# A two-layer attention kernel: float32r sums, a moved output, and a last projection in two parts

## The chip, the cores and the metric

The kernel runs on one core of a Trainium2 chip. The metric is the device time of one execution in microseconds (us); lower is better. The core's engines are called by the names that the profile uses: PE is TensorE (matmuls; PEld its weight loads), DVE is VectorE, ACT is ScalarE, POOL is GpSimd, and SP is SyncE, which in this kernel only starts DMAs.

## The reference

Eight images of 32 x 32 positions and 512 channels go through two layers. Each layer is a group norm (32 groups of 16 channels), an attention and a residual. Everything is float32.

```python
x = x + L0(gn(x))          # 16 heads of 32: softmax(q k^T / sqrt(32)) v, then w_proj, b_proj
x = x + L1(gn(x))          # 4 heads of 128, then Wo

# L1, for each image (1024 tokens):
q = x @ Wq * scale; k = x @ Wk; v = x @ Wv
scores = q k^T + pos       # pos: relative logits from q and pos_emb_w, pos_emb_h
out = softmax(scores) @ v @ Wo
```

The softmax's denominator, a sum over 1024 keys for each head and query, is what the first part of the change touches.

## The kernel before

**Layout.** Activations lie with features on the partitions: an image is four chunks of 128 channels x 1024 tokens, in one of eight equal buffers ("block"). Logits are computed transposed, keys on the partitions and queries along the row, so the sum over keys runs over partitions. DVE therefore adds the exp tiles of the eight key blocks of a head into one tile `esum` (128 x 512 queries, L675 and L677), and TensorE multiplies that with a matrix of ones, which gives the sum in every partition.

**Projections.** Each of the ten or so 512 x 512 projections of an image uses a Strassen-Winograd form: instead of eight products of half size there are seven (`seven`, order 0, 5, 1, 4, 6, 2, 3), for each half `u` of the output features. `forms` makes on DVE, in four subtractions or additions (L339 to L342), the combinations of the four quarters of the activations; products 0 and 1 use raw quarters (`a11`, `a12`). A product is eight matmuls of 128 x 32 columns (`by_columns`, L315), four of them side by side in the array. Sinks (`Plain`, `Onto`) put the products' sums where they belong, with ACT copies (L374, L393), DVE adds (L379, L443) and POOL adds (L438). The weights, or sums of them, come by a planned stream of loads on SP's queue (`Stream`, L193 and L197); `Matrix.add_up` makes the summed weights once (L146) and stores them to DRAM.

**PSUM.** Eight banks: four are one tile "ps" (the layer-0 logits, four heads at once), three are "bank", one is "acc".

**Order of the work.** In the main loop pass b runs the layer-0 attention of image b (512 steps) and puts between its steps a list of other work: the end of layer 0 of image b−1 (`after_0`), the last projection of layer 1 of image b−2 (`after_1`, ending in `put_out`: transpose, then four stores for each tile, L856 and L861) together with the second norm of b−1, then q, k, v and the position logits of layer 1 of b−1 (`second`), its attention (`attention_1`), and the projections of layer 0 of b+1. The loading and first norm of b+1 (`load`) is woven between the steps of `attention_1`, one part every six steps (`woven(..., 4, 6)`). The steps of `attention_1` have cost 0 to the interleaver, so a whole second-layer attention normally runs within one step of the first-layer attention, and the "ps" banks are unused meanwhile. Only in the pass of the last image do the first 32 of its 64 steps alternate with layer-0 steps. The last pass has the second layer of image 7 alone, and after it the last projection, `after_1(7)`. A scheduler, which estimates durations, then decides each engine's final order within what the dependencies allow.

**A second-layer attention** has 4 heads x 2 halves of the queries, each of eight key blocks. A step (`front`, `back`) is a matmul q k (L654), a float32r matmul that adds the position logits (L655), an exp on ACT (L657), a matmul with v into "acc" (L666) and the DVE addition to `esum`. After the eighth, ACT copies acc to q's place (L680) and `finish` makes the sum:

```python
su = bank(f"sums_{name}")
nc.tensor.matmul(su, ones, esum, start=True, stop=True)     # L686
normalise(q[:, h, c * NB : (c + 1) * NB], su, name)
```

`normalise` copies it on ACT (L502), transposes it on DVE so that the reciprocal works on 16 columns (L504, L507), makes a check (L510), transposes back (L520) and multiplies on POOL (L524). These small tiles share tag "rec" with two buffers.

**The start** (`load_first`): image 0 is read in rows and transposed by TensorE; ACT and DVE copy the chunks out of PSUM (L752, L754); six idle matmuls follow; DVE takes statistics in chunk order 1, 0, 3, 2; `put_away` stores the four chunks to DRAM on SP's queue (L218); the group norm overwrites them in place (L294). The summed weights of the first projections are made on POOL and DVE (L146).

At the end of the kernel a flag is computed from the checks (L1014 to L1018): a slower general path would follow if a sum were out of bounds.

Of the kernel before, what the change touches and what calls it, by code (L numbers as in the profile page):

```python
# [17 lines left out]
P = 128  # L18
# [9 lines left out]
def quick_path(  # L28
# [55 lines left out]

    ident = consts.tile([P, P], F32, tag="ident", name="ident")
    make_identity(nc, ident)
    ones = consts.tile([P, P], F32, tag="ones", name="ones")
    nc.gpsimd.memset(ones, 1.0)
    bproj_sb = consts.tile([P, CC], F32, tag="bproj_sb", name="bproj_sb")
    with nc.allow_non_contiguous_dma(reason="512 values, once"):  # L90
        nc.gpsimd.dma_start(bproj_sb, b_proj.rearrange("(cc p) -> p cc", p=P))
# [71 lines left out]


    ORDER = [0, 5, 1, 4, 6, 2, 3]

    class Stream:

# [138 lines left out]

    begun = [None]
    half_done = [None]

    def by_columns(out, weights, moving, start, stop, open_sum=False):

# [11 lines left out]
                tc.keep_in_program_order(ins)  # L324
        in_place[0] = False

    def forms(x, name, room=None):


        a11, a12 = x[:, :HC, :NB], x[:, HC:, :NB]  # L330
        a21, a22 = x[:, :HC, NB:], x[:, HC:, NB:]
        if room is not None:
            s1, s2, s4 = [room[:, i, :].rearrange("p (c n) -> p c n", n=NB) for i in range(3)]
        else:
            s1, s2, s4 = [
                mem.tile([P, HC, NB], F32, tag=f"form{i}", name=f"f{i}_{name}", bufs=1)
                for i in (1, 2, 4)
            ]
        nc.vector.tensor_add(s1, a21, a22)  # L339
        nc.vector.tensor_sub(s2, s1, a11)  # L340
        nc.vector.tensor_sub(a21, a11, a21)
        nc.vector.tensor_sub(s4, a12, s2)  # L342
# [5 lines left out]
    def seven(fs, u, rows, sink, name, hook=None):  # L348

        def product(out, i, start):
            w, f = stream.take(i), fs[i]
            if not rows:
                for c in range(HC):
                    by_columns(out, w[c], f[:, c, :], start and c == 0, c == HC - 1, True)
            else:
                for t in range(2):
                    for c in range(HC):  # L360
                        by_columns(
                            out[:, t * HN : (t + 1) * HN],
                            f[:, c, (2 * u + t) * P : (2 * u + t + 1) * P],
                            w[c],
                            start and c == 0 and t == 0,
                            c == HC - 1,
                            True,
                        )
            stream.ahead()

        x = bank(f"x_{name}")
# [7 lines left out]
        begun[0] = nc.vector.tensor_add(a, y, p1)  # L379
# [23 lines left out]
        yield HC  # L403

    class Plain:

# [234 lines left out]
                if i % 2:  # L641
                    yield 0

    def attention_1(q, k, v, posT, b):

        steps = [(h, c, j) for h in range(H1) for c in range(NH) for j in range(NT)]
        state = {}

        def front(h, c, j):
            name = f"1_{b}_{h}_{c}_{j}"  # L650
            ps = bank(f"ps_{name}")
            keys = slice(j * P, (j + 1) * P)
            queries = slice(c * NB, (c + 1) * NB)
            nc.tensor.matmul(ps, k[h][:, keys], q[:, h, queries], start=True, stop=False)  # L654
            nc.tensor.matmul(ps, sel_flat[:, keys], posT[:, h, queries], start=False, stop=True)  # L655
            e = mem.tile([P, NB], F32, tag="e1", name=f"e_{name}", bufs=3)
            nc.scalar.activation(e, ps, AF.Exp, scale=1.0 / math.sqrt(D1))  # L657
            return e

        def back(h, c, j, e):  # L660
            name = f"1_{b}_{h}_{c}_{j}"
            if j == 0:
                state["acc"] = bank(f"acc_{name}")
                state["first"] = e
            acc = state["acc"]
            nc.tensor.matmul(  # L666
                acc,
                v[:, j, h * D1 : (h + 1) * D1],
                e,
                start=(j == 0),  # L670
                stop=(j == NT - 1),
            )
            if j == 1:
                state["esum"] = mem.tile([P, NB], F32, tag="es1", name=f"es_{name}", bufs=2)
                nc.vector.tensor_add(state["esum"], state["first"], e)  # L675
            elif j > 1:
                nc.vector.tensor_add(state["esum"], state["esum"], e)  # L677
            if j < NT - 1:
                return
            nc.scalar.copy(q[:, h, c * NB : (c + 1) * NB], acc)  # L680
            state["ended"] = (h, c, state["esum"])

        def finish(h, c, esum):
            name = f"1_{b}_{h}_{c}"
            su = bank(f"sums_{name}")
            nc.tensor.matmul(su, ones, esum, start=True, stop=True)  # L686
            normalise(q[:, h, c * NB : (c + 1) * NB], su, name)

        pending = None
        for at in steps:  # L690
            e = front(*at)
            ended = state.pop("ended", None)
            if pending is not None:
                back(*pending)
            pending = (*at, e)
            if ended is not None:
                finish(*ended)
            yield 0
        back(*pending)
        yield 0  # L700
        finish(*state.pop("ended"))

    def load(b, st):

# [15 lines left out]
        yield 0  # L720
        st["kept"] = put_away(xT, f"0_{b}")
        yield from group_norm(st, xT, f"0_{b}")
        st["xn"] = forms(x, f"xn0_{b}")
        yield 0

    def load_first(st):

# [7 lines left out]
        for h in range(NH):  # L735
# [6 lines left out]
            for t in range(NT // NH):  # L742
                for cc in range(CC):
# [2 lines left out]
                        rows[:, h * (NT // NH) + t, cc * P : (cc + 1) * P],  # L746
                        ident,
                    )
            for cc in range(CC):
                part = xT[cc][:, h * NB : (h + 1) * NB]  # L750
                if h == 0 or cc % 2:
                    nc.scalar.copy(part, banks[cc])  # L752
                else:
                    nc.vector.tensor_copy(part, banks[cc])  # L754

        idle = psum.tile([P, CC, NB], F32, tag="ps", name="idle", bufs=1)
        for t in range(6):
# [86 lines left out]

    def after_1(b, st, hook=None):

        if "ao1" not in st:
            forms_1(b, st)
        fs = st.pop("ao1")
        xT = fetch(st["kept"], block(f"x2T_{b}"))  # L850
        for u in range(2):

            def put_out(n, h):
                m = n * HC + u
                ot = mem.tile([P, NB], F32, tag="row", name=f"ot_{b}_{m}_{h}", bufs=3)
                nc.vector.transpose(ot, xT[m][:, h * NB : (h + 1) * NB])  # L856
                ot = ot.rearrange("p (t i) -> p t i", i=32)
                for a in range(P // 32):

                    queue = nc.scalar if b == B - 1 and a % 2 else nc.sync  # L860
                    queue.dma_start(  # L861
                        by_blocks(of[b, h * NB : (h + 1) * NB, :], m * P + 32 * a),
                        ot[32 * a : 32 * a + 32],
                    )

            stream.unit(WO, False, u)
            yield from seven(
                fs, u, False, Onto(halves(xT, u), then=put_out), f"wo_{b}_{u}", hook if u else None
            )

    def woven(main, side, start, gap, places=(0,)):

# [51 lines left out]
    for b in range(B + 1):  # L924
# [10 lines left out]
    plan += units(WO)  # L935
# [22 lines left out]
    for b in range(B + 1):  # L958
# [11 lines left out]
        if last is not None:  # L970
# [14 lines left out]
            attention = later(lambda st: attention_1(*st.pop("at")), last)  # L985
            if here is not None and coming is None:

                attention = woven(
                    (int(at < H1 * NT) for at, _ in enumerate(attention)),
# [513 lines left out]
```

## Time and profile before

| | |
|---|---|
| three timed runs | 3873.93, 3877.97, 3879.32 us; median 3877.97 |
| the profiled execution | 3877.0 us, of which the traced span is 3875.2 us |
| granted TensorE clock, mean | 0.996 of full speed |
| DVE, largest lines | L569 893.3 us (layer-0 sums), L677 290.6 us, 384 times, 757 ns each |
| ACT, largest lines | L547 961.6 us (layer-0 exp), L657 305.7 us, 512 times, 597 ns each |
| float32 sums of layer 1, L686 | 64 sums as 128 matmul records, 593 ns each |

Busy times of a line are sums of durations, and a share of 98% says that an engine nearly always had something in work. Matmuls are pipelined: the record of a matmul lasts longer than the distance to the next one, so what a matmul costs is read from the distance of starts, not from its duration. A float32 matmul has two records. The waits view lists, for an engine, the idle time before its instructions and what ended it; the timeline lists instructions in order of start, with that idle time in brackets.

### The profile page before, as it was taken

The numbers are of one execution on the slowest core, as the hardware profiler recorded it, in microseconds if no ns is written. First come the engines' busy times: TensorE is split into PE (matmuls) and PEld (weight loads), VectorE is DVE, ScalarE is ACT, GpSimd is POOL, SyncE is SP. The second block draws the span as 40 slices with busy tenths as digits, with TensorE's granted clock in tenths as the row PEclk, the third lists the DMA queues.
The fourth block names the chain that finished last, engine by engine and source line by source line (L and its number), as shares of the span: only waits on it lengthen the run. The fifth ranks groups of instructions, "written<-read, shape, count | busy, mean of one in ns | idle before, by whom it ended". The sixth has DMA issues, their size and how long they took to land.

```text
span 3875.2 us, 79813 instructions
## 1 busy us (share of the span) xinstructions
PE 3803.0 (98%) x34478; PEld 1375.0 (35%) x34478; DVE 2516.4 (65%) x2905; ACT 1723.9 (44%) x1767; POOL 625.1 (16%) x400
## 2 busy tenths in 40 slices
PE   8999999999999999999999999999999999999998
PEld 3222244232443234432343323433234332334353
DVE  6777765686745867468664686656866568665544
ACT  2554543545434454344544445444453445553232
POOL 2242101121001211012111121111210112001101
PEclk9999999999999999999999999999999999999999
DMA  6122120142202322033120241103311023110401
GB/s 183 58 87 80 42 60 3 37 126 65 57 6 79 94 54 55 12 92 87 42 55 17 92 94 38 47 21 98 90 41 39 27 97 76 34 52 24 121 17 23
DMA packets 482984, 234.73 MB, mean 61 GB/s; under 512 B 269600, under 2 KB 461376, under 8 KB 481600
## 3 DMA queue, kind: packets, MB, share of 16 engines
q1 hardware_dynamic: 470992, 213.74, 20.4%
q0 software_dynamic: 2608, 13.70, 1.0%
q8 instruction: 274, 4.49, 0.5%
q10 hardware_dynamic: 9024, 2.10, 0.3%
q14 instruction: 86, 0.70, 0.1%
HBM read 170.72 MB, written 58.72 MB: 59 GB/s over the span
## 4 chain that ended last, share of the span: by engine, by line
PE 87%; DVE 8%; ACT 2%; issue 2%; DMA 0%; SPq 0%; POOL 0%; DVEq 0%; ACTq 0%; POOLq 0%
PE ps L539 12%; PE ps L654 11%; PE acc L666 11%; PE acc L558 11%; PE y_q L315 4%; PE y_v L315 4%; PE y_k L315 4%; PE ps L655 3%; PE x_q L315 3%; PE z_k L315 3%; PE x_v L315 3%; PE x_k L315 3%; PE z_q L315 3%; PE z_v L315 3%; DVE es L569 2%; ACT e L547 2%
## 5 line engine op out<-in xcount | busy, mean ns | idle before, releaser
L547 ACT ACTIVATE e<-ps 128x2048 f32<-128x2048 f32 x512 | 961.6, 1878 | 839.3 <-PE ps L539 628.2
L569 DVE TENSOR_TENSOR es<-es,e 128x2048 f32<-128x2048 f32 x384 | 893.3, 2326 | 408.6 <-ACT e L547 405.6
L539 PE MATMUL ps<-q,k 32*64 32x512 f32 x8192 | 576.6, 614 | 18.4 <-ACT e L547 18.4
L657 ACT ACTIVATE e<-ps 128x512 f32<-128x512 f32 x512 | 305.7, 597 | 573.8 <-PE ps L655 537.8
L558 PE MATMUL acc<-e,v 128*32 128x512 f32 x4096 | 545.9, 605 | 0.0
L654 PE MATMUL ps<-q,k 128*128 128x512 f32 x1024 | 525.2, 595 | 0.3 <-DVE posT L640 0.3
L666 PE MATMUL acc<-e,v 128*128 128x512 f32 x1024 | 522.0, 593 | 0.0
L524 POOL TENSOR_TENSOR q<-q,su 128x512 f32<-128x512 f32 x128 | 216.3, 1690 | 1556.8 <-DVE su L520 1538.0
L677 DVE TENSOR_TENSOR es<-es,e 128x512 f32<-128x512 f32 x384 | 290.6, 757 | 252.8 <-ACT e L657 250.8
L655 PE MATMUL ps<-posT,sel 128*128 128x512 f32 x512 | 407.0, 795 | 0.0
L654 PEld LDWEIGHTS ps<-q,k 128*128 128x128 f32 x1024 | 192.9, 190 | 250.4 <-issue 243.8
L539 PEld LDWEIGHTS ps<-q,k 32*64 32x64 f32 x8192 | 120.3, 130 | 409.8 <-issue 221.1
L666 PEld LDWEIGHTS acc<-e,v 128*128 128x128 f32 x1024 | 193.5, 190 | 146.3 <-issue 105.0
L558 PEld LDWEIGHTS acc<-e,v 128*32 128x32 f32 x4096 | 81.5, 108 | 412.0 <-issue 364.7
L567 DVE TENSOR_TENSOR es<-e,e 128x2048 f32<-128x2048 f32 x64 | 172.9, 2701 | 33.2 <-ACT e L547 33.2
L504 DVE STREAM_TRANSPOSE tu<-su 128x512 f32<-128x512 f32 x128 | 90.6, 708 | 121.7 <-ACT su L502 120.1
L502 ACT COPY su<-sums 128x512 f32<-128x512 f32 x128 | 74.9, 585 | 149.0 <-PE sums L579 81.2
L655 PEld LDWEIGHTS ps<-posT,sel 128*128 128x128 f32 x512 | 97.5, 190 | 122.3 <-issue 122.3
L640 DVE TENSOR_TENSOR posT<-pp,posT 32x512 fp32r<-32x512 f32 x128 | 112.0, 875 | 32.3 <-ACT posT L635 31.0
L675 DVE TENSOR_TENSOR es<-e,e 128x512 f32<-128x512 f32 x64 | 44.2, 691 | 135.8 <-ACT e L657 135.8
L428 POOL TENSOR_TENSOR k<-b_k,p_k 128x512 f32<-128x512 f32 x32 | 51.9, 1623 | 483.6 <-ACT p_k L393 483.6
L635 ACT CAST posT<-pp 32x512 fp32r<-32x512 f32 x128 | 106.2, 829 | 46.3 <-PE pp L622 45.1
(200 smaller groups left out, 4449.4 us busy)
## 6 DMA issues: line engine op xcount, KB each, us to landing
w_qkv<-ws_qkv SPq DMA_DIRECT2D x168, 128.0 KB, 2.5
d<-x0T SPq DMA_DIRECT2D x32, 512.0 KB, 3.6
x1T<-d SPq DMA_DIRECT2D x32, 512.0 KB, 5.4
d<-x1T SPq DMA_DIRECT2D x32, 512.0 KB, 3.4
x2T<-d SPq DMA_DIRECT2D x32, 512.0 KB, 6.0
w_qkv<-in_L_conv_w_qkv SPq DMA_DIRECT2D x126, 128.0 KB, 2.2
out<-ot SPq DMA_DIRECT2D x240, 64.0 KB, 2.0
xs<-in_x SPq DMA_DIRECT2D x224, 64.0 KB, 2.5
```

The costliest lines, as they stand in the source:

```text
L315: ins = nc.tensor.matmul(out[columns, :], weights[:, columns], moving, start=start, stop=stop, skip_group_check=open_sum,)
L524: nc.gpsimd.tensor_tensor(dst, dst, su, op=ALU.mult)
L539: nc.tensor.matmul(ps[some, r, :], k[m][rows, j * P + 64 * i : j * P + 64 * i + 64], q[m][rows, h * NB : (h + 1) * NB], start=True, stop=True,
L547: nc.scalar.activation(e, ps, AF.Exp, scale=D0 ** -0.5)
L558: nc.tensor.matmul(acc[r * D0 : (r + 1) * D0, :], v[:, j, c0 : c0 + D0], e[:, r, :], start=(j == blocks[0]), stop=(j == blocks[-1]),)
L567: nc.vector.tensor_add(state["esum"], state["first"], e)
L569: nc.vector.tensor_add(state["esum"], state["esum"], e)
L654: nc.tensor.matmul(ps, k[h][:, keys], q[:, h, queries], start=True, stop=False)
L655: nc.tensor.matmul(ps, sel_flat[:, keys], posT[:, h, queries], start=False, stop=True)
L657: nc.scalar.activation(e, ps, AF.Exp, scale=1.0 / math.sqrt(D1))
L666: nc.tensor.matmul(acc, v[:, j, h * D1 : (h + 1) * D1], e, start=(j == 0), stop=(j == NT - 1),)
L677: nc.vector.tensor_add(state["esum"], state["esum"], e)
```

## The change

1. `ones` becomes a float32r tile. In `attention_1.finish` the sum of a head is split: ACT copies `esum` to float32r (`greater`), DVE subtracts that from `esum` (`rest`), and some steps later two float32r matmuls add both into a tile of the "ps" banks. `normalise` is the same. Only where the layer-0 attention of the last image alternates with the steps (`beside` = 32, that is for the first three sums of image 6) does the single float32 matmul into a "bank" stay. The sum at the very end of each attention is made at once, in all its parts.
2. `forms` becomes a generator, `forming`; in `load` its four operations are spread over four parts, each held behind the latest `esum` addition, and `load` gets a part every five steps.
3. At the start all eight copies out of PSUM are on ACT, in chunk order 0, 2, 1, 3, as are the statistics; the summing of the query and key weights of layer 0 is held behind the last of the forms.
4. The output of image 6 (`put_out`) is put off: its eight transposes with their stores come between the steps of the last attention.
5. The last projection of image 7 (`after_last`) makes products 0 and 1 for both halves u first, from raw quarters, then the forms, then the other five products for both halves; the plan of weights follows that order.

```diff
-    ones = consts.tile([P, P], F32, tag="ones", name="ones")
-    nc.gpsimd.memset(ones, 1.0)
+    ones_r = consts.tile([P, P], F32R, tag="ones", name="ones")
+    nc.gpsimd.memset(ones_r.bitcast(F32), 1.0)
+    ones = ones_r.bitcast(F32)
...
+    FIRST_TWO, LAST_FIVE = [0, 1], [5, 4, 6, 2, 3]
...
-    def forms(x, name, room=None):
+    def forming(x, name, room=None, behind=None):
...
+            late = behind() if behind is not None else None
+            with tc.issue_after(late.ins) if late is not None else nullcontext():
+                last_form[0] = op(out, one, other)
+            yield 0
...
+    def two_first(fs, u, sink, name):
+        product = taken(fs, u, False)
+        x = bank(f"x_{name}")
+        product(x, 0, True)
+        p1 = snapshot("e1", f"p1_{name}")
+        nc.scalar.copy(p1, x)
+        product(x, 1, False)
+        sink.c11(x)
+        return p1
+
+    def five_last(fs, u, sink, name, p1):
+        product = taken(fs, u, False)
+        y = bank(f"y_{name}")
+        product(y, 5, True)
+        a = snapshot("es1", f"a_{name}")
+        nc.vector.tensor_add(a, y, p1)
+        sink.early(p1, a)
...
         def finish(h, c, esum):
             name = f"1_{b}_{h}_{c}"
-            su = bank(f"sums_{name}")
-            nc.tensor.matmul(su, ones, esum, start=True, stop=True)
+            if (h * NH + c + 1) * NT < beside:
+                su = bank(f"sums_{name}")
+                nc.tensor.matmul(su, ones, esum, start=True, stop=True)
+                normalise(q[:, h, c * NB : (c + 1) * NB], su, name)
+                return
+            yield
+            greater = mem.tile([P, NB], F32R, tag="rec", name=f"sg_{name}", bufs=2)
+            nc.scalar.copy(greater, esum)
+            rest = mem.tile([P, NB], F32R, tag="rec", name=f"sr_{name}", bufs=2)
+            nc.vector.tensor_sub(rest, esum, greater.bitcast(F32))
+            yield
+            yield
+            su = psum.tile([P, HB, NB], F32, tag="ps", name=f"sums_{name}", bufs=1)[:, 0, :]
+            nc.tensor.matmul(su, ones_r, greater, start=True, stop=False)
+            nc.tensor.matmul(su, ones_r, rest, start=False, stop=True)
             normalise(q[:, h, c * NB : (c + 1) * NB], su, name)
...
-        finish(*state.pop("ended"))
+        run(finish(*state.pop("ended")))
...
-        st["xn"] = forms(x, f"xn0_{b}")
-        yield 0
+        st["xn"] = yield from forming(x, f"xn0_{b}", behind=lambda: added[0])
...
-            for cc in range(CC):
+            for cc in (0, 2, 1, 3):
                 part = xT[cc][:, h * NB : (h + 1) * NB]
-                if h == 0 or cc % 2:
-                    nc.scalar.copy(part, banks[cc])
-                else:
-                    nc.vector.tensor_copy(part, banks[cc])
+                nc.scalar.copy(part, banks[cc])
...
-        for cc in (1, 0, 3, 2):
+        for cc in (0, 2, 1, 3):
             statistics(st, xT, cc, "0_0")
...
+            late = b == B - 2
+            with tc.issue_after(added[0].ins) if late else nullcontext():
+                nc.vector.transpose(ot, xT[m][:, h * NB : (h + 1) * NB])
...
+    def late_output(st):
+        for put in st.pop("late"):
+            put()
+            yield 0
+
+    def after_last(b, st):
+        x = st["ao"]
+        xT = fetch(st["kept"], block(f"x2T_{b}"))
+        sinks = [Onto(halves(xT, u), then=put_out(b, st, xT, u)) for u in range(2)]
+        early = [x[:, :HC, :NB], x[:, HC:, :NB]]
+        p1s = []
+        for u in range(2):
+            stream.unit(WO, False, u)
+            p1s.append(two_first(early, u, sinks[u], f"wo_{b}_{u}"))
+        fs = forms(x, f"ao1_{b}")
+        for u in range(2):
+            stream.unit(WO, False, u)
+            five_last(fs, u, sinks[u], f"wo_{b}_{u}", p1s[u])
...
-        m.add_up(nc.vector, nc.gpsimd, keep=True)
+
+        with tc.issue_after(last_form[0].ins):
+            m.add_up(nc.vector, nc.gpsimd, keep=True)
...
-            rest.append(woven(attention, incoming, 4, 6))
+            if here is None:
+                incoming = later(late_output, past)
+            rest.append(woven(attention, incoming, 4, 5))
...
-    run(after_1(B - 1, states[B - 1]))
+    after_last(B - 1, states[B - 1])
```

More of the change, by code (lines that the diff above doesn't have):

```diff
@@ L309, in quick_path @@
     half_done = [None]
+    last_form = [None]
+    added = [None]
     def by_columns(out, weights, moving, start, stop, open_sum=False):
@@ L338, in forms, with whole, taken @@
             ]
[L339 to L342, printed above, removed]
-        return [a11, a12, s4, a22, s1, s2, a21]
+        for op, out, one, other in (
+            (nc.vector.tensor_add, s1, a21, a22),
+            (nc.vector.tensor_sub, s2, s1, a11),
+            (nc.vector.tensor_sub, a21, a11, a21),
+            (nc.vector.tensor_sub, s4, a12, s2),
+        ):
+            late = behind() if behind is not None else None
+            with tc.issue_after(late.ins) if late is not None else nullcontext():
+                last_form[0] = op(out, one, other)
+            yield 0
+        return [a11, a12, s4, a22, s1, s2, a21]
+    def forms(x, name, room=None):
+        got = []
+        def whole():
+            got.append((yield from forming(x, name, room)))
+        run(whole())
+        return got[0]
     def snapshot(tag, name):
         return mem.tile([P, NB], F32, tag=tag, name=name, bufs=3 if tag == "e1" else 2)
-    def seven(fs, u, rows, sink, name, hook=None):
+    def taken(fs, u, rows):
         def product(out, i, start):
@@ L369, in product, with seven @@
             stream.ahead()
+        return product
+    def seven(fs, u, rows, sink, name, hook=None):
+        product = taken(fs, u, rows)
         x = bank(f"x_{name}")
@@ L403, in seven @@
         yield HC
+    def two_first(fs, u, sink, name):
[14 more added lines that the diff above has]
+        sink.early(p1, a)
+        product(y, 4, False)
+        b = snapshot("es1", f"b_{name}")
+        nc.vector.tensor_add(b, y, p1)
+        sink.middle(b)
+        z = bank(f"z_{name}")
+        product(z, 6, True)
+        p7 = snapshot("e1", f"p7_{name}")
+        nc.scalar.copy(p7, z)
+        product(y, 2, False)
+        sink.c12(y, p1)
+        product(z, 3, False)
+        sink.c21(z, a)
+        sink.c22(b, p7)
     class Plain:
@@ L642, in position_logits, with attention_1 @@
                     yield 0
-    def attention_1(q, k, v, posT, b):
+    def attention_1(q, k, v, posT, b, beside=0):
         steps = [(h, c, j) for h in range(H1) for c in range(NH) for j in range(NT)]
@@ L676, in back @@
             elif j > 1:
[L677 removed]
+                added[0] = nc.vector.tensor_add(state["esum"], state["esum"], e)
             if j < NT - 1:
@@ L684, in finish @@
             name = f"1_{b}_{h}_{c}"
-            su = bank(f"sums_{name}")
-            nc.tensor.matmul(su, ones, esum, start=True, stop=True)
+            if (h * NH + c + 1) * NT < beside:
[13 more added lines that the diff above has]
+            nc.tensor.matmul(su, ones_r, rest, start=False, stop=True)
             normalise(q[:, h, c * NB : (c + 1) * NB], su, name)
         pending = None
+        ending = []
         for at in steps:
             e = front(*at)
-            ended = state.pop("ended", None)
             if pending is not None:
@@ L695, in attention_1 @@
             pending = (*at, e)
-            if ended is not None:
-                finish(*ended)
+            for part in ending:
+                next(part, None)
+            if "ended" in state:
+                ending = [finish(*state.pop("ended"))]
+                next(ending[0], None)
             yield 0
@@ L845, in after_1 @@
     def after_1(b, st, hook=None):
-        if "ao1" not in st:
-            forms_1(b, st)
         fs = st.pop("ao1")
@@ L851, in after_1 @@
         for u in range(2):
[L853 to L864, printed above, removed]
@@ L866, in after_1, with put_out, put, put_later @@
             stream.unit(WO, False, u)
             yield from seven(
-                fs, u, False, Onto(halves(xT, u), then=put_out), f"wo_{b}_{u}", hook if u else None
-            )
+                fs, u, False, Onto(halves(xT, u), then=put_out(b, st, xT, u)), f"wo_{b}_{u}",
+                hook if u else None,
+            )
+    def put_out(b, st, xT, u):
+        def put(n, h):
+            m = n * HC + u
+            ot = mem.tile([P, NB], F32, tag="row", name=f"ot_{b}_{m}_{h}", bufs=3)
+            late = b == B - 2
+            with tc.issue_after(added[0].ins) if late else nullcontext():
+                nc.vector.transpose(ot, xT[m][:, h * NB : (h + 1) * NB])
+            ot = ot.rearrange("p (t i) -> p t i", i=32)
+            for a in range(P // 32):
+                queue = nc.scalar if b == B - 1 and a % 2 else nc.sync
+                queue.dma_start(
+                    by_blocks(of[b, h * NB : (h + 1) * NB, :], m * P + 32 * a),
+                    ot[32 * a : 32 * a + 32],
+                )
+        def put_later(n, h):
+            st.setdefault("late", []).append(lambda: put(n, h))
+        return put_later if b == B - 2 else put
@@ L934, in quick_path @@
             plan += FIRST if b else units(WQ0) + units(WK0)[:1] + units(WV0, True)
-    plan += units(WO)
+    plan += [(WO, False, u, some) for some in (FIRST_TWO, LAST_FIVE) for u in range(2)]
     states = [{} for _ in range(B)]
@@ L984, in quick_path @@
             total += SECOND
-            attention = later(lambda st: attention_1(*st.pop("at")), last)
-            if here is not None and coming is None:
+            shared = here is not None and coming is None
+            attention = later(
+                lambda st, steps: attention_1(*st.pop("at"), steps), last, H1 * NT if shared else 0
+            )
+            if shared:
                 attention = woven(
```

## The prediction

> **What bounds the kernel now.** I read the head of the page first: busy time by engine, the clock strip, the chain that ended last.
>
> ```profile
> span 3875.2 us, 79813 instructions
> PE 3803.0 (98%) x34478; PEld 1375.0 (35%) x34478; DVE 2516.4 (65%) x2905; ACT 1723.9 (44%) x1767; POOL 625.1 (16%) x400
> PEclk9999999999999999999999999999999999999999
> PE 87%; DVE 8%; ACT 2%; issue 2%; DMA 0%; SPq 0%; POOL 0%; DVEq 0%; ACTq 0%; POOLq 0%
> ```
>
> TensorE is busy 98%, at full clock, and carries the chain. So an edit pays where it takes matmuls out of TensorE's queue, or where it closes one of TensorE's few waits. The waits view, taken for TensorE, lists those:
>
> ```profile
> PE ps L539 <- ACT e L547: 18.4, 16, 2.9
> PE x_v L315 <- issue: 10.6, 1, 10.6
> PE y_wo L315 <- DVE a_wo L379: 10.5, 7, 1.7
> PE y_wo L315 <- DVE f_ao L340: 3.1, 1, 3.1
> PE x_q L315 <- DMA w_q<-in_L_conv_Wq: 2.9, 1, 2.9
> ```
>
> (total, times, longest). All waits come to some 60 us; the largest stays. The matmul side is read from the timeline of a second-layer attention (start, duration, engine, line, operation, output<-inputs, shape, count; in brackets, further on, the idle time before it and what ended that):
>
> ```profile
> 3717.66 1.02 PE L654 MATMUL ps<-q,k 128*128 128x512 f32 x2
> 3718.74 1.02 PE L666 MATMUL acc<-e,v 128*128 128x512 f32 x2
> 3719.60 1.02 PE L686 MATMUL sums<-es,ones 128*128 128x512 f32 x2
> 3720.46 1.02 PE L654 MATMUL ps<-q,k 128*128 128x512 f32 x2
> ```
>
> Durations overlap, so starts count: a float32 128x512 matmul (two records) takes 0.86 us (3719.60 to 3720.46). Plain steps start 1.947 us apart (3704.03 to 3705.98) and hold two of those and the float32r matmul of L655: 1.947 − 2×0.859 = **0.228 us** for one float32r matmul of the same shape.
>
> **A. Sums inside the heads.** 64 sums; 3 of batch 6 stay as they were, 8 end an attention (below); 53 change from 0.859 to 2×0.228 us: 53 × 0.403 = **−21.3 us**. New on ACT: a copy, 0.585 us by L502's row, on DVE a subtraction, 0.69 by L675's. In the changed program's order the copy stands between the exp of step 7 and that of the next head's step 0. After the last logits of a head the exp takes 0.6, the es add 0.7, the copy 0.6, the next exp 0.6: done at about +2.75 us; TensorE wants that exp after acc, logits, acc, logits, at +3.9. So 1.1 us of cover; were it gone, each us of delay is a us on TensorE. The sums stand two to three steps later and wait for nothing. The pair could be dearer than 0.456: each loads its own weights, 0.19 us in L655's row, beside the matmul before. Bounds: no gain (0.43 each, as a float32 record), and −22.9 at 0.213. I take L655's row, the same operation between the same neighbours. The Trainium skill, "FP8 and Floating Point Precision", TensorE Precision Notes, has true float32 in four passes through the array; 0.859/4 = 0.215 a pass, so a pair of single passes would be the −22.9. It prices no float32r, and the row says 0.228.
>
> **B. Ends of attentions 0 to 6.** Here the change adds a wait. Before, the sum follows the last es add:
>
> ```profile
> 1144.71 0.69 DVE L677 TENSOR_TENSOR es<-es,e 128x512 f32<-128x512 f32 x1 [1.26 <-ACT e L657]
> 1145.69 1.02 PE L686 MATMUL sums<-es,ones 128*128 128x512 f32 x2
> 1146.64 1.92 PE L315 MATMUL x_q<-x0T,w_qkv 128*32 128x512 f32 x16
> ```
>
> After it, one x_q matmul of eight goes first, then the pair, then seven x_q. Es ready 1145.40; copy to 1146.02; subtraction to 1146.75; second matmul about 1147.06 to 1147.28; seven x_q in two rounds of four column groups, 1.72: 1149.0, against 1148.3 before: 0.7 each, 7 × 0.7 = **+5 us**. A rule speaks against the change here: "TensorE: Matmul & The Clock Gate", Step-by-step: only weight loads are pulled ahead, matmuls stay in program order. Could x_q pass the waiting pair, the end would gain 0.4 (−3 us); the trace, where x_q ready long before follows the sum, agrees with the rule. Bounds 0 to +7.
>
> **C. Half-size sums.** The float32 sums of batch 6 that stay are issued a step earlier; in the changed order two of them cut a group of eight layer-0 logits matmuls (32x64 tiles, side by side in one round of 0.86) into one and seven: one more round each, **+1.7 us** (0 to +3, should the es add be late).
>
> **D. Start.** TensorE's first product waits here:
>
> ```profile
> 26.36 2.98 DVE L294 TENSOR_SCALAR x0T<-x0T,back,rstd 128x1024 f32<-128x1024 f32 x4 [1.17 <-POOL rstd L290]
> 27.28 3.64 PE L315 MATMUL x_v<-prep_qkv,x0T 128*32 128x256 f32 x32 [10.57 <-issue]
> ```
>
> With copies on ACT and eight weight sums (0.65 each by L146's rows) held behind the forms, the statistics no longer queue on DVE. But L294 overwrites x0T, which four 512 KB stores read; the key weights' fetch (1 MB, 2.5 us at the 410 GB/s of that stretch) now precedes them on SP. They land about 25 to 27 instead of 22.3. The forms gain 2 to 4 us, then a_v waits behind the held sums, so the fourth product starts near 37 as before with about 2 us more work done: **−2 us** (0 to −6). A later store of summed weights delays the loads queued on SP by some 10 us; they are wanted over 60 us later.
>
> **E. Output of batch 6.** Its eight transposes and 32 stores now lie between the last projection of that batch and the next products:
>
> ```profile
> 3607.08 1.92 PE L315 MATMUL y_wo<-f_ao,w_o 128*32 128x512 f32 x16 [1.74 <-DVE a_wo L379]
> 3622.43 4.13 SPq L861 DMA_DIRECT2D out<-ot  x8
> 3629.09 3.62 PE L315 MATMUL x_q<-x1T,w_q 128*32 128x512 f32 x16 [2.92 <-DMA w_q<-in_L_conv_Wq]
> ```
>
> SP spends 0.52 us on each store, and w_q's loads stand behind them. Moved away: 1.74 (a_wo no longer behind transposes), 2.92, and 3.62 − 1.92 = 1.7 of clock lost to the pause (0.80 granted there): **−6.3 us** (−3 to −7; the first a_wo wait, 1.63, stays). Where they go, between the steps of the last attention, DVE idles 1.25 us of each step and gets 0.7; SP has nothing behind them that is wanted before the tail, since w_o and x2T are ahead of them.
>
> **F. Tail.**
>
> ```profile
> 3836.80 2.27 DVE L339 TENSOR_TENSOR f_ao<-q 128x1024 f32<-128x1024 f32 x1 [1.10 <-POOL q L524]
> 3840.39 3.31 PE L315 MATMUL y_wo<-f_ao,w_o 128*32 128x512 f32 x16 [3.14 <-DVE f_ao L340]
> 3863.08 1.90 PE L315 MATMUL z_wo<-q,w_o 128*32 128x512 f32 x14
> ```
>
> From the last acc (end 3831.6) to the last product's end (3864.7): 33.1 us for 14×1.72 + 0.86 = 24.9 of work; the rest is 0.75, 3.14, about 2 of slow clock, 2 of small waits. After: the sums come 0.65 later, but four raw products (6.9) run over normalisation and forms, with perhaps 1.7 of waits for their copies; the third kind starts near 3841.8, a_wo behind forms and transposes costs 1.1, ten products 17.2 less what overlaps: end about 3861.3, **−3.5 us** (−1 to −6). Cover gone (copies late by one product): 1.7 back. The clock gate section of the same page wants about 3.4 us of idleness before it halves the clock; 3.14 idle went with 0.83 in 3840 to 3850. By either a pause under 1 us keeps the clock. What follows the last product (adds, transposes, stores, 10.5 us) stays.
>
> **Sum.** −21.3 + 5 + 1.7 − 2 − 6.3 − 3.5 = −26.4. Span 3875.2 becomes 3849. The profiled execution took 3877.0, 1 below the median shown, 3877.97; so the median goes to **3852 us**.
>
> **Rivals.** *Float32r pairs save nothing*: A is 0 (weight loads of the pair and of its neighbours not hidden). For: L655 never stands as a pair of loads on one accumulation, and its 0.795 us of duration is long. Against: 0.228 as spacing in every step of the timeline. Result 3878 − 5 = 3873, no change. *The sums pay, the edges don't*: stores of x0T land late, DVE's order in the tail takes the gain; D, E, F give −3 instead of −11.8: 3860, still faster. *Slower*: the copy delays the next head's exp. Its place is ACT's queue at a head's end; it waits for DVE's es add, and during the next batch's load DVE also has transposes (0.7) and forms (1.2 to 2.3). From 1.1 us late on, TensorE waits; the 53 heads pay back the −26 at 0.5 us each, that is at 1.6 us late on average; at 2 us late, +48 − 26 = 3900. Against: of the waits above none is acc's on DVE or ACT, L677 idles 253 us before its adds, and only some heads have a form before them. *The change doesn't do what it says*: the scheduler puts the sums back; its order doesn't show that.
>
> **Chances.** Forecast and near it 0.66; edges fail 0.19 (3855 to 3866); pairs save nothing 0.09; slower 0.06. A measurement tells 0.2% (7.8 us) from no change. So faster 0.85, same 0.09, slower 0.06. Range 3841 (all ends good: −22.9, 0, 0, −6, −7, −6 is 3836, unlikely together) to 3867, into the second rival.
>
> **What will show it.** Sums at float32r spacing: two starts 0.23 apart and a step of 2.40 where it was 2.80; x_q after an attention's end starting near 1147 relative to the old times; no 2.92 wait for w_q; the first f_ao wait under 1 us. A new line "acc waits for ACT e L657" of over 10 us would mean the slower rival; sums spaced 0.43, the first.

## The result, and the profile after

The changed kernel takes 3853.27 us (median; 3852.96 to 3854.03) against 3876.78 us before (3873.93 to 3879.32): 23.5 us less, a ratio of 0.9942 (95% interval 0.9929 to 0.9956). The forecast was 3852, in a range of 3841 to 3867. The profiled execution has a span of 3852.2 us against 3875.2.

The page of the changed kernel starts with

```profile
span 3852.2 us, 79876 instructions
PE 3793.3 (98%) x34478; PEld 1376.7 (36%) x34478; DVE 2555.5 (66%) x2964; ACT 1760.4 (46%) x1830; POOL 620.8 (16%) x400
```

TensorE is still the bound. DVE and ACT have got 39 and 37 us more work, as the split adds 61 operations to each, and inside the heads of the attentions all but 0.6 us of it stays hidden behind TensorE; at their ends it doesn't (below). The waits of TensorE (total, times, longest):

```profile
PE ps L596 <- ACT e L604: 18.7, 16, 2.9
PE y_wo L320 <- DVE a_wo L404: 8.7, 6, 1.6
PE x_v L320 <- issue: 5.4, 1, 5.4
PE y_wo L320 <- DVE a_wo L446: 1.0, 1, 1.0
PE acc L723 <- ACT e L714: 0.3, 1, 0.3
```

Gone are the 2.9 us for w_q's DMA and the 3.1 for f_ao; the first product waits 5.4 instead of 10.6. Among the new ones, all small, are a_wo in the tail (L446) and one acc that waits for an exp: the last row is the mechanism of the slower rival, in one place.

Where the time went is best read by places. The second-layer attentions are good marks: for each, the start of its first and of its last logits in both traces. "Inside" is the change of what lies between; a "gap" is that from one attention's last logits to the next one's first.

| place | forecast | before to after, us |
|---|---|---|
| start, to the first layer-0 logits (65 us) | −2 | −2.35 |
| start, to the first second-layer attention (537 us) | | −1.64 |
| inside, images 1 to 5 and 7, seven split sums each | −2.82 | −2.71 to −2.72 |
| inside, image 0 | −2.82 | −2.13 |
| inside, image 6 | +0.1 | +0.84 |
| gaps after images 0 to 5 | +0.7 | +0.70 to +0.82 |
| gap after image 6 (output moved away, one end) | −5.6 | −5.89 |
| from the last logits to the end | −3.5 | −2.49 |

A step with sums, in the timeline of the last attention of the changed kernel:

```profile
3704.82 1.02 PE L723 MATMUL acc<-e,v 128*128 128x512 f32 x2
3705.27 0.79 PE L759 MATMUL sums<-sg,ones 128*128 128x512 f32 x1
3705.90 0.39 PE L760 MATMUL sums<-sr,ones 128*128 128x512 f32 x1
3706.13 1.02 PE L711 MATMUL ps<-q,k 128*128 128x512 f32 x2
```

The logits before these started at 3703.73, so the step takes 2.40 (2.42 in most heads) where it took 2.80: the pair costs 0.45 to 0.47 us, the forecast being 0.456. Note how the first record starts before acc is done: starts of single records mislead, the distance from logits to logits doesn't.

### The profile page after: what moved, and what is told of

Its sections match the earlier page's. It is cut to its first block, busy times and chain, and to the rows that moved or that the text cites. A ratio compares the mean times of both kernels' runs of the same rounds, so it can differ in the third digit from the quotient of the medians.

```text
span 3852.2 us, 79876 instructions
## 1 busy us (share of the span) xinstructions
PE 3793.3 (98%) x34478; PEld 1376.7 (36%) x34478; DVE 2555.5 (66%) x2964; ACT 1760.4 (46%) x1830; POOL 620.8 (16%) x400
## 5 line engine op out<-in xcount | busy, mean ns | idle before, releaser
L485 POOL TENSOR_TENSOR v<-b_v,p_v 128x512 f32<-128x512 f32 x32 | 51.6, 1614 | 440.0 <-ACT p_v L418 431.9
```

## The experiments

### The split taken back

```diff
-            if (h * NH + c + 1) * NT < beside:
+            if True:
+                yield
                 su = bank(f"sums_{name}")
                 nc.tensor.matmul(su, ones, esum, start=True, stop=True)
```

> All 64 sums of the second layer are single float32 matmuls in a bank again, at the step where the kernel before has them; the rest of the change stays. My sum says that the split is worth 0.39 us in each of 53 heads less 0.75 at each of 7 ends, less 2.4 in image 6: the inside of an attention returns to +2.72 us, the ends to -0.77 each, and the span goes from 3852.2 to about 3865 (+13). If the gain came from elsewhere (the other bank, the finer forms), it stays near 3852.

Measured: span 3863.4, median 3863.81 us. Every inside is within 0.01 us of the kernel before, every gap between images 0 and 6 within 0.12. So the split alone makes both the gain inside and the loss at the ends, and is worth 11.3 us net. The finer forms of part 2 stayed in this run, so by themselves they give no time inside; whether the split needs them was not tried. The start (−1.60 to the first attention) and the gap after image 6 (−6.66) stay. The tail, which I had not counted here, went to −3.40: a single float32 sum at the very end is 0.9 better than the pair.

### Only the ends taken back, and the ends put off

The first edit makes the last sum of each attention one float32 matmul at once. The second keeps the pair for images 0 to 5 but issues it after two products of the next projection:

```diff
# ends_f32
-            if (h * NH + c + 1) * NT < beside:
+            if (h * NH + c + 1) * NT < beside or (h, c) == (H1 - 1, NH - 1):
# ends_deferred
...
-        run(finish(*state.pop("ended")))
+        last_sum[0] = finish(*state.pop("ended"))
+        if b >= B - 2:
+            run(last_sum[0])
...
+            rest.append(woven(before, after_products(), 0, 1))
```

> Only the last sum of each attention is a single float32 matmul again, at once; the 53 inner ones stay split. If the waiting pair costs the 0.77 us that the trace shows between attentions, seven of these go and the span is 3852.2 - 5.4 = 3846.8 (with the tail up to 1 less). If that 0.77 belongs to something else at the ends (the later x_q, a bank), nothing moves.

> The last sum of attentions 0 to 5 stays a float32r pair, but is issued after the first two products of the next projection instead of before them (images 6 and 7: single float32 at once). If matmuls queue strictly behind a waiting one, and the pair itself costs 0.47 us against 0.86, the six ends gain 0.77 + 0.39 each against the changed kernel: about -7 there and -1.5 for images 6 and 7, near 3843.5. If the cost is the pair itself and not its wait, it is equal to the changed kernel.

Measured: 3847.76 and 3848.01 us, spans 3845.1 and 3845.6. The first is the forecast: each of seven gaps gets back 0.75 to 0.88, the tail 0.95. The second is a miss: it expected another 0.39 at each of six ends, and got nothing at five; at the end of image 0 it even lost 0.9 against the first, as the pair put off there cut a group of eight logits matmuls into one and seven (at 668.91 and 670.91). The end of image 1's attention in the changed kernel:

```profile
1139.03 0.69 DVE L734 TENSOR_TENSOR es<-es,e 128x512 f32<-128x512 f32 x1 [1.26 <-ACT e L714]
1139.81 0.62 ACT L751 CAST sg<-es 128x512 fp32r<-128x512 f32 x1 [0.81 <-DVE es L734]
1140.11 1.04 PE L320 MATMUL x_q<-x0T,w_qkv 128*32 128x512 f32 x2
1140.53 0.69 DVE L753 TENSOR_TENSOR sr<-es,sg 128x512 fp32r<-128x512 f32 x1 [0.81 <-ACT sg L751]
1141.08 0.50 PE L759 MATMUL sums<-sg,ones 128*128 128x512 f32 x1
1141.42 0.40 PE L760 MATMUL sums<-sr,ones 128*128 128x512 f32 x1
1141.75 1.92 PE L320 MATMUL x_q<-x0T,w_qkv 128*32 128x512 f32 x14
```

One x_q matmul has a round of the array for itself (0.86 us, in which four could run side by side), then comes the pair, whose second half follows sr (done at 1141.22), then the other seven, as the forecast had it. With a float32 sum there, and with the pair put off:

```profile
1138.73 1.02 PE L744 MATMUL sums<-es,ones 128*128 128x512 f32 x2
1139.68 1.93 PE L320 MATMUL x_q<-x0T,w_qkv 128*32 128x512 f32 x16
```

```profile
1144.51 0.50 PE L763 MATMUL sums<-sg,ones 128*128 128x512 f32 x1
1144.85 0.39 PE L764 MATMUL sums<-sr,ones 128*128 128x512 f32 x1
1145.17 1.92 PE L321 MATMUL x_q<-x0T,w_qkv 128*32 128x512 f32 x16
```

Between products of 32-column matmuls the pair waits for nothing and still takes 0.66 us from its start to the next product's, and that start is 0.11 after the product before would have made room. Within an attention it costs 0.47. From the start of the last two acc matmuls to the start of the second x_q product the two arrangements differ by 0.09 us (8.26 with the float32 sum, 8.17 with the pair put off). So the saving of a pair, 0.39, holds among 128-column matmuls; between 32-column ones 0.09 of it is left. Whether its weight loads or the change of shape take the difference isn't told apart here.

### The sums of image 6 that stay float32

```diff
             if (h * NH + c + 1) * NT < beside:
+                yield
                 su = bank(f"sums_{name}")
```

> The three float32 sums that stay in image 6 are issued a step later, where the kernel before has them; all else stays changed. If the cut groups of eight layer-0 logits cause the loss in image 6, its attention shortens from +0.84 us against before to about -1.6 (four split sums at -0.39 each), the span to about 3849.8. If the loss comes from the switch to split sums after step 32, nothing moves.

Measured: 3850.57 us, span 3848.2; inside image 6 −1.55, all other insides as in the changed kernel. What it takes away, in the changed kernel:

```profile
3413.13 1.07 PE L596 MATMUL ps<-q,k 32*64 32x512 f32 x2
3414.12 1.12 PE L744 MATMUL sums<-es,ones 128*128 128x512 f32 x2
3417.13 1.11 PE L596 MATMUL ps<-q,k 32*64 32x512 f32 x14
```

One logits matmul of eight takes a round, 0.99 us to the sum's start, and the other seven another. A second group is cut in the same way at 3438.46. Together this costs 2.39 us; the forecast said 1.7, without the 0.1 us at each change of shape.

### The output of image 6 put back

```diff
-        return put_later if b == B - 2 else put
+        return put
...
-            late = b == B - 2
+            late = False
```

> The output of image 6 is transposed and stored as its projection makes it, as before; all else stays changed. My step E says +6.6 us, all of it between the attentions of images 6 and 7: the wait of w_q for its DMA (2.9) back, one a_wo wait (1.7) back, a slow clock (1.7). The rival that DVE or the stores hinder the last attention would show there a gain when they leave: attention 7 shorter than 127.8 - 2.7 us by a measurable amount.

Measured: 3860.47 us, span 3858.9 (+6.68), of which +6.59 in the gap after image 6 and 0.01 inside attention 7. The eight transposes thus cost nothing between the last attention's steps. Among TensorE's waits the old row of a_wo is back, and that for w_q is larger than before:

```profile
PE y_wo L320 <- DVE a_wo L404: 10.5, 7, 1.7
PE x_q L320 <- DMA w_q<-in_L_conv_Wq: 3.4, 1, 3.4
```

### The last projection in one part

```diff
-    plan += [(WO, False, u, some) for some in (FIRST_TWO, LAST_FIVE) for u in range(2)]
+    plan += units(WO)
...
-    after_last(B - 1, states[B - 1])
+    forms_1(B - 1, states[B - 1])
+    run(after_1(B - 1, states[B - 1]))
```

> The last projection of image 7 runs as before (forms first, then seven products for each half), its last sum stays a pair. The two-part projection was worth 3.4 us in the two runs whose last sum is a single float32 matmul, and the pair takes 0.9 of that; so the tail should go from -2.5 to about +0.9 us against before, the span from 3852.2 to 3855.6. If the tail is set by the stores at the end, it stays at 3852.

Measured: 3856.67 us, span 3855.7; the tail goes to +1.22 against before (+3.71 against the changed kernel). The two parts are worth 3.71, which is near what was expected of them; and the waiting pair costs 1.22 in the old tail. In the changed kernel's tail the raw products still wait, twice for an ACT copy of the product before (the first copy ends at 3815.45), and then y_wo for a_wo:

```profile
3814.87 0.58 ACT L436 COPY p_wo<-x_wo 128x512 f32<-128x512 f32 x1 [1.28 <-PE x_wo L320]
3815.55 3.64 PE L320 MATMUL x_wo<-q,w_o 128*32 128x512 f32 x30 [0.73 <-issue]
3819.89 1.92 PE L320 MATMUL x_wo<-q,w_o 128*32 128x512 f32 x16 [0.69 <-ACT p_wo L436]
3826.30 2.33 PE L320 MATMUL y_wo<-f_ao,w_o 128*32 128x512 f32 x17 [1.01 <-DVE a_wo L446]
```

With the float32 sum at the end (ends_f32) three of them run without a pause, and one wait of 1.43 for f_ao is left.

### The start: the hold and the copies

```diff
# not_held
-        with tc.issue_after(last_form[0].ins):
-            m.add_up(nc.vector, nc.gpsimd, keep=True)
+        m.add_up(nc.vector, nc.gpsimd, keep=True)
# copies_old
-                nc.scalar.copy(part, banks[cc])
+                if h == 0 or cc % 2:
+                    nc.scalar.copy(part, banks[cc])
+                else:
+                    nc.vector.tensor_copy(part, banks[cc])
...
-        for cc in (0, 2, 1, 3):
+        for cc in (1, 0, 3, 2):
             statistics(st, xT, cc, "0_0")
```

> The sums of the query and key weights are not held behind the forms at the start; copies and statistics stay on their new engines and orders. By my step D the held sums only move DVE's work from before the forms to before a_v, and the stores of x0T set the normalisation anyway: the stretch up to the first second-layer attention stays within 1 us of -1.6 against before. If the hold is what gains, all 1.6 go.

> Copies out of PSUM and the order of the statistics at the start as before (two on DVE; order 1, 0, 3, 2), the weight sums still held behind the forms. The stores of x0T, not the statistics, end the normalisation in the changed kernel, so the stretch up to the first second-layer attention stays at -1.6 us within 1: about 3853. If the copies and their order gain by themselves, it loses 1.6 or more.

Both missed. Without the hold 3857.82 us, and 5.1 later than the changed kernel at the first layer-0 logits: the weight sums stand between the steps of the group norm again, and its last step ends at 30.8 instead of 27.8. Some 2 of the 5.1 may be the clock's, which stays at half until 37.79 (30.46 in the changed kernel) while DVE waits for a product:

```profile
37.68 0.69 DVE L404 TENSOR_TENSOR a_v<-y_v,p_v 128x512 f32<-128x512 f32 x1 [2.11 <-PE y_v L320]
```

With the old copies 3850.82 us, and 2.7 earlier there. But that run has a second difference: the key weights' fetch again follows the stores on SP. What this is worth is seen on DVE in the changed kernel (three of four chunks):

```profile
20.54 0.81 DVE L296 TENSOR_SCALAR x0T<-x0T,back,rstd 128x1024 f32<-128x1024 f32 x1 [1.66 <-DMA d<-x0T]
23.22 0.81 DVE L296 TENSOR_SCALAR x0T<-x0T,back,rstd 128x1024 f32<-128x1024 f32 x1 [0.74 <-DMA d<-x0T]
26.96 0.81 DVE L296 TENSOR_SCALAR x0T<-x0T,back,rstd 128x1024 f32<-128x1024 f32 x1 [2.93 <-DMA d<-x0T]
```

The normalisation waits for the four stores, chunk by chunk. The last lands at 26.94; in copies_old at 21.81. So the order on SP makes the start slower, not the copies on ACT: the last version below keeps these copies, puts only the fetch back, and its normalisation ends at 22.99, earlier than in copies_old (23.78). Step D had named this queue and the landing time, and then priced only the net.

### Where the cover of the exp ends

One or three DVE operations are put before each float32r copy, and the next head's first exp is held behind that copy, where ACT has it in the changed kernel too; the copy of acc follows that exp. In held1 and held3 three heads of image 6 are copied from acc after their normalisation and leave unnormalised, so image 6 isn't used. Each is a single execution.

```diff
+            for _ in range(3):                       # 1 in held1
+                nc.vector.tensor_tensor(esum, esum, esum, op=ALU.max)
...
+            with tc.issue_after(copy.ins) if copy is not None else nullcontext():
+                nc.scalar.activation(e, ps, AF.Exp, scale=1.0 / math.sqrt(D1))
```

> One more DVE operation of about 0.69 us (a maximum of the sums with themselves, which leaves them as they are) stands before the float32r copy of every split sum, and the next head's first exp is held behind that copy on ACT. My cover for that exp is 1.1 us: 0.7 is inside it, so the inside of the attentions stays at -2.7 us against before, and only the ends lose, 7 x 0.7: about 3857. If there is no such cover, 53 heads lose 0.7 each: about 3894.

> The same with three such operations, about 2.0 us. By a cover of 1.1 us each head then loses 0.9 to 1.0 us: +48 to +53 inside, +15 at the ends, about 3917, which is slower than before the change. If the exp is not on the way (the rival of no danger), only the ends lose: about 3867.

Measured: 3864.97 and 3920.38 us, spans 3863.2 and 3918.6. With three, one head of image 1:

```profile
1070.53 2.14 DVE L753 TENSOR_TENSOR es<-es 128x512 f32<-128x512 f32 x3
1072.76 0.62 ACT L755 CAST sg<-es 128x512 fp32r<-128x512 f32 x1 [2.99 <-DVE es L753]
1073.28 0.59 ACT L718 ACTIVATE e<-ps 128x512 f32<-128x512 f32 x1
1073.93 1.13 PE L727 MATMUL acc<-e,v 128*128 128x512 f32 x2
```

Such a head takes 0.92 us more for 2.18 of delay: the cover is 1.26 us, the forecast 1.1. The insides of images 1 to 5 grow by 8.0 us each (seven heads, three of which have other DVE work in their way too), all eight by 62.5 where 48 to 53 was expected. The gaps together grow by nothing, as the order around them changed (+2.1 after image 0, −0.4 to −0.6 after images 1 to 5), and the tail by 5.6, where +15 was expected of the ends. So the total, +66 us against some +65, agrees in part by luck. The kernel is slower than before the change, as the rival had it. The run with one operation is a miss. It adds 0.7; five heads of image 1 lose nothing, as forecast, but one loses 0.2 and one 1.4 (the insides of images 1 to 5 grow by 1.6 each where nothing was expected, the ends by nothing where 0.7 was):

```profile
1107.82 1.22 DVE L353 TENSOR_TENSOR f_xn<-f_xn,x0T 128x1024 f32<-128x1024 f32 x1
1108.96 0.69 DVE L753 TENSOR_TENSOR es<-es 128x512 f32<-128x512 f32 x1
1109.73 0.62 ACT L755 CAST sg<-es 128x512 fp32r<-128x512 f32 x1 [2.55 <-DVE es L753]
```

A form of the coming image stands before the added operation, 1.22 us, and the two together pass the cover. So the rival was real, and near: the changed kernel meets it once, in image 0, where the last norm operation and an es add come late, acc waits 0.3 us, and a step takes 2.55 instead of 1.95. That is the 0.6 by which image 0 falls short:

```profile
580.41 2.49 DVE L296 TENSOR_SCALAR x0T<-x0T,back,rstd 128x1024 f32<-128x1024 f32 x2
584.38 0.62 ACT L751 CAST sg<-es 128x512 fp32r<-128x512 f32 x1 [2.42 <-DVE es L734]
585.55 1.13 PE L723 MATMUL acc<-e,v 128*128 128x512 f32 x2 [0.33 <-ACT e L714]
```

### The other bank

```diff
-            su = psum.tile([P, HB, NB], F32, tag="ps", name=f"sums_{name}", bufs=1)[:, 0, :]
+            su = bank(f"sums_{name}")
```

> The split sums go into one of the three tiles named bank instead of the unused four-bank tile. If the other bank only spares a wait for a free one, a step with sums takes longer than 2.42 us, by up to 0.5: +5 to +25 us inside the attentions. If three banks are enough, as the kernel before suggests (a step with sums had no wait there), the inside stays at -2.72 and only the order at the ends moves, within 1 us each.

Measured: 3855.83 us, span 3853.3; every inside within 0.02 of the changed kernel. The unused bank gives nothing inside the attentions. The 2.6 us between the medians are not explained by the span's 1.1 (0.5 in the gap after image 6, 0.7 in the tail, where the order differs).

### A version that beats both

> Four edits at different places: the last sum of each attention single float32, at once (measured -7.1 with the tail); the float32 sums of image 6 a step later (measured -2.4); at the start the key weights' fetch behind the stores of x0T on SP (my step D: the stores land 2 us earlier, up to -1.5); the flag's matmul behind the last product in the tail (-0.6 to -1). Sum about -11.5: span 3840.7, and faster than both kernels. If the places share a cause, less than -9.4.

```diff
-            if (h * NH + c + 1) * NT < beside:
+            if (h * NH + c + 1) * NT < beside or (h, c) == (H1 - 1, NH - 1):
+                if (h * NH + c + 1) * NT < beside:
+                    yield
...
-        m.fetch(nc.sync)
+        with tc.issue_after(stored[0].ins) if m is WK0 else nullcontext():
+            m.fetch(nc.sync)
...
-    nc.tensor.matmul(pf, ones, bad, start=True, stop=True)
+    with tc.issue_after(last_mm[0].ins):
+        nc.tensor.matmul(pf, ones, bad, start=True, stop=True)
```

Measured: 3842.25 us (3840.34 to 3843.41), ratio to the kernel before 0.9912 (0.9898 to 0.9925), span 3839.2. The sum is right, its terms less so. With the fetch behind the stores the first layer-0 logits come 4.2 us earlier, not 1.5: the last store lands at 21.67, and the normalisation runs in one piece.

```profile
20.01 2.98 DVE L296 TENSOR_SCALAR x0T<-x0T,back,rstd 128x1024 f32<-128x1024 f32 x4 [1.17 <-POOL rstd L292]
```

The clock may help here: it is at half for 3.4 us from 20.57, in the changed kernel for 10.2. How much of the 4.2 this gives isn't told apart. The flag's matmul was a miss: the last product starts 30.8 us after the last logits with it or without (in ends_f32 the product behind it would have waited for b_wo anyway). The last two transposes start 2.90 us after that in both, but the last store lands 11.5 us after it instead of 10.4: stores started 3.64 us after it land at 8.86, in ends_f32 at 6.84. Why isn't shown. Without that edit a little more may be had; this was not tried.

## Why the prediction was right

- **A** (−21.3): right in kind, close in size. 0.389 us for each inner sum, by the runs with and without the split; less 0.6 in image 0. About −20.
- **B** (+5): right. 0.77 a gap, seven times. The float32 sum at the ends takes away just this.
- **C** (+1.7): right in kind, +2.39 in size: a cut group of narrow matmuls costs its round and about 0.1 us at each change of shape.
- **D** (−2): right at −2.35 up to the first logits, and by the path that was named (a_v behind the held sums, at 37.30), but from two larger terms that I had not sized: the hold, worth up to −5.1 with the clock's share in it (+2.8 against before without it); and the fetch ahead of the stores, which takes back up to 4.2. That these come out near −2 is in part luck. Naming the queue wasn't enough; it had a price.
- **E** (−6.3): right, −6.6, all its terms seen: the DMA wait, one a_wo wait, and the slow clock.
- **F** (−3.5): right in kind, −2.5 in size. By tail_old the late pair alone costs 1.22 where 0.65 was set, and the two parts gain 3.71 where 3.5 + 0.65 was set. a_wo's wait (1.0) and the copies' (0.73 and 0.69) came as foreseen, and the clock stayed full over them.
- The first rival fell with the pair's 0.47 us, the second with the start, E and F, which together give −10.7 (−1.6, −6.6, −2.5) and not −3. The slower one has its mechanism shown (held3), its point at 1.26 us, and one occurrence in the changed kernel.

The span's −23.0 is 3.4 short of the sum of −26.4: 1.3 in A, 0.7 in C, 1.0 in F, 0.4 each in B and the start, against −0.3 in E. The median came nearer, 3853.27 against 3852, and that is luck: the forecast counted from 3877.97, and with a fourth run the median before is 3876.78.

## What to carry to other kernels

A price read from one row holds among the same neighbours: the same pair costs 0.47 us between wide float32 matmuls and 0.66 or more between narrow ones, so a last iteration deserves its own sum. Where an operation's cost is "hidden", work out by how much (here 1.26 us), and see which other work shares its queue at that time. And a transfer moved ahead of others on one queue is priced by what then lands late, even if nobody waits for the transfer itself.

## What the runs showed of the hardware

A pause of TensorE well under 3.4 us can halve its clock, and the same pause in another run doesn't. In image 0 of the changed kernel TensorE waits 1.85 us for an exp and starts again at 380.78. Windows of the changed kernel, then of beside_step, whose order is the same there (span of the window; busy time of PE, PEld, DVE, ACT, POOL; granted clock; DMA share; GB/s):

```profile
380.00:384.00 4.00, 3.22 (x28) 0.83 (x32) 3.24 (x3) 2.60 (x2) 0.00 (x0) 0.75 0.12 35
384.00:388.00 4.00, 4.00 (x39) 1.00 (x31) 4.00 (x5) 0.58 (x1) 0.00 (x0) 0.82 0.07 20
```

```profile
380.00:384.00 4.00, 3.21 (x36) 0.92 (x40) 3.23 (x3) 2.62 (x2) 0.00 (x0) 1.00 0.12 35
384.00:388.00 4.00, 4.00 (x48) 1.04 (x44) 4.00 (x5) 1.09 (x2) 0.00 (x0) 1.00 0.21 58
```

The first trace loses 1.68 us here. This is why beside_step, which changes nothing before image 6, comes to its first second-layer attention 1.68 us sooner than the changed kernel. In the records the clock is at half for 3.4 us from 382.0, in the one trace and not in the other; other stretches at half last 6.8, 10.2 or 17.1 us, twice to five times that. The Trainium skill, "TensorE: Matmul & The Clock Gate", What's actually happening, tells of a window of 3413 ns that runs free and doesn't start with the kernel; stretches in multiples of 3.4 us, and a pause that counts in one run and not in the next, agree with it, but 1.85 us is less than the idle window of about 3.4 that it names. The fourteen traces show the steps: in each, the starts of the stretches at half lie whole multiples of 3.413 us apart, to within 0.01 (in the changed kernel 20.22, 146.51, 330.83 and 382.03). Counted in these steps, the pause of 1.85 us lies wholly inside one step in six traces, and in five of these the next step is at half; in the other eight a boundary cuts the pause, into a longer part of at most 1.82 us, and the clock stays. Why the sixth (ends_deferred) escapes isn't shown. So one such pause is worth its own length and, by chance of where it falls, 1.7 us more. At the start of best the clock is at half for 3.4 us instead of the changed kernel's 10.2, and in E and in the tail a stretch of 3.4 us at half went with the waits.
